# A block of attention, experts and rotation on one core: other loads first, extra products while they run, one add and five columns moved

## The chip, the cores and the metric

The kernel runs on one core of a Trainium2 chip. Five engines of the core work side by side, each with its own instruction stream: TensorE (PE in the profile; PEld is its weight load), VectorE (DVE), ScalarE (ACT), GpSimd (POOL) and SyncE (SP), which here issues transfers. They wait for each other through semaphores. The metric is the device time of one execution in microseconds (us). The time before is 677.72 us, the median of 3 runs (677.05 to 679.04).

## The reference

x has 4 sequences of 512 tokens with 288 channels; cond has one row of 288 for each sequence.

```python
mod = silu(c) @ w_adaln + b_adaln                      # (4, 1728)
sh_msa, sc_msa, g_msa, sh_mlp, sc_mlp, g_mlp = split(mod, 6)
h = ln(x) * (1 + sc_msa) + sh_msa
q, k, v = split(h @ w_qkv + b_qkv)                     # 16 heads of 18
o = softmax(q k^T * 18**-0.5) v @ w_proj + b_proj
x = x + g_msa * o
xn = ln(x) * (1 + sc_mlp) + sh_mlp
cw = softmax over the two largest of xn @ w_gate       # 4 experts
moe = sum_e cw_e * (gelu(xn @ w1_e + b1_e) @ w2_e + b2_e)   # 288 -> 1152 -> 288
x = x + g_mlp * moe
U, _ = qr(P)                                           # P is 288 x 64
R = expm(skew(silu(cond) @ W.T + b))                   # 64 x 64, one per sequence
z = x @ U
out = x + (z @ R - z) @ U.T
```

All of it is computed in float32.

## The kernel before

Everything happens in `fast_path`. The order of the instructions of each engine is the order in which the Python code emits them (a manual schedule), so "behind" on an engine always means later in the code. Each float32 matmul shows as two records (passes) in the profile, each transpose as one.

**Start (L983 to L1100, L2267 to L2285).** SP issues the loads of `cs` (the condition), `wada` (the first 576 columns of w_adaln, 648 KB, one transfer), four tiles of `xs` (the first sequence, 144 KB each), `raw` (part of w_qk, two transfers) and `wadb` (the rest of w_adaln, 1296 KB). ACT's queue issues `badT` (the bias, turned by the host) and the q and k bias. GpSimd fills constants until 6.83 us. `first()` makes the moments of x on DVE (L1180, L1181) and the inverse spread `rs` on GpSimd (L1193, L1194). `shift_scale` makes shift and scale in the layout channel x sequence: for each of the two, 9 products with a 96x96 block of `wada` as weights and 4 columns, into `pm`, and one DVE add into `modT` (L1097); between the two DVE normalizes x (`norm`, L1216). Then ACT compacts two items of w_qk (L1048, L1052); `other_heads` loads the rest of w_qk into the space of `wada`; for each of 3 channel blocks `modulate_T` turns the normalized x with 4 transposes into `pt` (L1229), and ACT applies `modT` into `hT` (L1232); `project` multiplies `hT` by the compacted weights into `pq` (L1787), ACT copies that to `row` (L1829), and SP sends it to `qk`, one transfer for each head (L1834). `values` are the products `pv` (L1750). `qks` are four tiles of 128x2x512, zeroed by DVE, two of them at the very start (L1059).

**Attention (L2428 to L2526).** 32 pairs of steps, 8 for each sequence. A step makes scores `z` (L1865), their exponentials on ACT (L1874) and their products with the values `av` (L1885). A plan hangs other pieces on each pair, in slots `a`, `s` and `b`: the projections of the next sequence, the output projection, the routing, and `column`, the next column of a Householder factorization of P on DVE (`triangular`, L1601 to L1646), 66 pieces in all with the first and the last. Pieces of the matrix exponential (`rotations`, with the squarings L1480, L1530) come one by one beside the pairs. A piece that is a `Split` has a product that `ahead()` can emit before the pair: the first Split of the next pair's `a` and `s` is led so (L2515).

**Experts (L2831 to L2878).** Tokens are sorted by expert into `slots` in two halves; eight expert passes follow, each with `hidden` (L2592, L2605) and `outputs` (L2652), whose rows GpSimd scatters to `chosen` (L2668). At every yield of these, one piece of the list `rest` is emitted: first what is left of the routing, then all columns that are left, then empty steps, then the products that end the factorization (`basis`, L1675 to L1721) with the first half's adds.

**Tail (L2882 to L2892).** Eight pairs of token tiles, four of each half. `Finish.load` reads the two chosen rows of each token (`ycl`, 128x2x2x288 for a pair, 576 KB). `Finish.add` adds them (L2716), multiplies by the gate (L2718) and adds x (L2719), all on DVE; `turn` (L2727), `project_` (L2738) and `store` (L2753, L2761) rotate and write. For pair 4 (`Finish.PAIRS`) loads and adds are cut in two.

Of the kernel before, what the change touches and what calls it, by code (L numbers as in the profile page):

```python
# [10 lines left out]
F32 = mybir.dt.float32  # L11
I32 = mybir.dt.int32
AF = mybir.ActivationFunctionType
ALU = mybir.AluOpType
# [4 lines left out]
P = 128  # L19
# [14 lines left out]
ROOT_SHIFT = float(0x1F3B58D5)  # L34
ROOT_PART = 0.24985


class Split:
    def __init__(self, lead, rest):
        self.lead, self.rest, self.led = lead, rest, None  # L40

    def ahead(self):
# [786 lines left out]
def fast_path(  # L829
# [126 lines left out]
    def bank(shape, name):  # L956

        banks[0] += 1
        if third and banks[0] % 3 == 0:
            return third[0].tile(shape, F32, tag="n", name=name)  # L960
        return ps_m.tile(shape, F32, tag="m", name=name)
# [9 lines left out]
    with ExitStack() as s1:  # L971
# [10 lines left out]
        cs = const.tile([CC, NK, B], F32, name="cs")  # L982
        nc.sync.dma_start(out=cs, in_=cT)  # L983
        wad = w_adaln.rearrange("(k p) f -> p k f", p=CC)
        wada = ada.tile([CC, NK, 2 * C], F32, tag="wa", name="wada")
        nc.sync.dma_start(out=wada, in_=wad[:, :, : 2 * C])
        badT = const.tile([CC, 6, NK], F32, name="badT")
        nc.scalar.dma_start(out=badT, in_=b_adalnT)
        HS = 7
        raw = ada.tile([CC + 1, NK, 2 * HS * HQ], F32, tag="raw", name="raw")  # L990
        braw = raw.rearrange("p k f -> p (k f)")[CC : CC + 1, : 2 * NG * P]
        nc.scalar.dma_start(out=braw, in_=b_qk.rearrange("(o p) t g -> o (p t g)", o=1))
        for t in range(NT):
            nc.sync.dma_start(out=xs[:, t, :], in_=x[0, ts(t, P), :])

# [89 lines left out]
        def shift_scale(between):  # L1085
            pm = bank([P, 2, NK, B], "pm")
            for i in range(2):
                for ch in range(NK):
                    for k in range(NK):
                        nc.tensor.matmul(  # L1090
                            pm[:CC, i, ch, :],
                            wada[:, k, ds(i * C + ch * CC, CC)],
                            sc[:, k, :],
                            start=(k == 0),
                            stop=(k == NK - 1),
                        )
                nc.vector.scalar_tensor_tensor(  # L1097
                    modT[:, i],
                    pm[:CC, i],
                    float(i),  # L1100
                    badT[:, i, :].unsqueeze(2).to_broadcast([CC, NK, B]),
                    ALU.add,
                    ALU.add,
                )
                if i == 0:
                    between()

        VROW = (NH - 1) * (HD + 1) + HQ  # L1110
# [114 lines left out]

        def modulate_T(b, which, xh, k, dst):
            pt = bank([P, N], f"pt{which}{b}{k}")
            for t in range(NT):
                nc.tensor.transpose(  # L1229
                    pt[:CC, ts(t, P)], xh[:, t, ds(k * CC, CC)], ident  # L1230
                )
            nc.scalar.activation(  # L1232
                dst[:CC, k, :],
                pt[:CC, :],
                AF.Identity,
                bias=modT[:, 2 * which, k, b : b + 1],
                scale=modT[:, 2 * which + 1, k, b : b + 1],
            )
# [495 lines left out]
        def begin(b):  # L1734
# [10 lines left out]
            def turn(k):  # L1745
                modulate_T(b, 0, xhs[b], k, hT)

# [15 lines left out]
            def values(pv, t):  # L1763
# [11 lines left out]
                norm,  # L1775
                [lambda k=k: turn(k) for k in range(NK)],
                [Split(lambda t=t: lead(t), lambda pv, t=t: values(pv, t)) for t in range(NT)],
# [491 lines left out]
        first()  # L2269
        shift_scale(norm)  # L2270
        for qk in qks[2:]:
            nc.vector.memset(qk, 0.0)
        compact(0, nc.scalar.copy)
        compact(1, nc.scalar.copy)
        other_heads()
        for piece in turns:
            piece()
        products, sends = project(0, 0, nc.sync)
# [149 lines left out]
        for b in range(B):  # L2428
            at = b * HALF
            last = b == B - 1  # L2430

            for p in {1: (6,), 2: (7,), 3: range(2, 6)}.get(b, range(8)):
                also(at + p, "a", column)
# [37 lines left out]
            also(at + (4 if 0 < b < B - 1 else 6), "a", lambda b=b: residual(b))  # L2471
            for p in {1: (0, 1, 3), 2: (0, 1, 3), 3: (0, 1, 6)}.get(b, ()):
                also(at + p, "b", column)
# [25 lines left out]
        for pair in range(PAIRS):  # L2499
# [15 lines left out]
            if pair + 1 < PAIRS - HALF + 2:  # L2515
                following = plan[pair + 1]["a"] + plan[pair + 1]["s"]
                for piece in [x for x in following if isinstance(x, Split)][:1]:
                    piece.ahead()
# [12 lines left out]
    with ExitStack() as s2:  # L2531
# [148 lines left out]
        class Finish:  # L2680
# [30 lines left out]
            @staticmethod  # L2711
            def add(i):
                yc = Finish.st[i]
                for j, n in ((0, 1), (1, 1)) if i == Finish.PAIRS else ((0, 2),):
                    m, xi = yc[:, ds(j, n), 0, :], xs[:, ds(2 * i + j, n), :]
                    nc.vector.tensor_add(m, m, yc[:, ds(j, n), 1, :])  # L2716
                    g = gates[:, 1, 2 * i // NT, :].unsqueeze(1).to_broadcast([P, n, C])
                    nc.vector.tensor_mul(m, m, g)  # L2718
                    nc.vector.tensor_add(xi, xi, m)  # L2719
# [265 lines left out]
```

## Time and profile before

| what | us |
|---|---|
| median of 3 runs | 677.72 |
| profiled execution | 681.86 |
| its span | 679.9 |
| PE busy | 654.3 |
| PE, first product | 6.84 |
| pq's first pass, pv's first pass | 15.58, 22.09 |
| first scores z | 28.02 |
| last expert product ends, about | 650.2 |
| last PE product starts | 672.45 |

The span runs from the first to the last recorded instruction or transfer of the profiled execution; the time around it is 1.96 us. Busy time counts a pass from its start to its modelled end, so passes overlap. A line of a timeline has start, duration, engine, line of code, operation, output and inputs, and in brackets the idle time before it and what ended it. In a table of windows the columns are the stretch, its length, busy time (with the number of instructions) of PE, PEld, DVE, ACT and POOL, the granted TensorE clock, the busy share of the DMA engines and GB/s.

### The profile page before, as it was taken

How to read it: one execution, taken by the hardware profiler on the slowest of the kernel's cores; microseconds unless marked ns; L12 is line 12 of the kernel's file. 1: busy time of each engine (PE TensorE's matmuls, PEld its weight loads, DVE VectorE, ACT ScalarE, POOL GpSimd, SP SyncE). 2: the span in 40 equal slices, each digit the busy share in tenths (PEclk: the TensorE clock that was granted, in tenths of full speed). 3: DMA queues.
4: the chain of work that ended last, by engine and by line, in shares of the span. 5: the costliest groups of instructions: out<-in, count | busy, mean ns of one | idle time of the engine just before them, and what ended most of it. 6: DMA issues, size and time to landing. Idle time of an engine off the chain costs nothing. (4 is left out here: it accounts for less than half of the span.)

```text
span 679.9 us, 11333 instructions
## 1 busy us (share of the span) xinstructions
PE 654.3 (96%) x3599; PEld 392.0 (58%) x3599; DVE 447.5 (66%) x2000; ACT 293.6 (43%) x469; POOL 245.8 (36%) x388
## 2 busy tenths in 40 slices
PE   5999999999999989999999999999999999999994
PEld 5533344433534334456777757777677676776762
DVE  4443859796699768565978988888888800152135
ACT  4368566765675545733353223232332322312231
POOL 4024688645352485601423653213023031240110
PEclk9999999999999999999999999999999999999999
DMA  9358423233312234461535423644063143550044
GB/s 215 84 164 216 130 86 71 76 106 78 96 56 59 67 112 121 120 164 64 148 70 166 140 96 114 164 136 118 10 183 79 65 132 70 172 158 21 18 150 147
DMA packets 71392, 75.47 MB, mean 111 GB/s; under 512 B 34316, under 2 KB 58610, under 8 KB 71322
## 3 DMA queue, kind: packets, MB, share of 16 engines
q1 hardware_dynamic: 59910, 47.76, 25.3%
q0 software_dynamic: 10912, 26.47, 13.3%
q8 instruction: 30, 0.49, 0.3%
q10 hardware_dynamic: 500, 0.42, 0.3%
q14 instruction: 40, 0.33, 0.2%
HBM read 52.13 MB, written 18.23 MB: 103 GB/s over the span
## 5 line engine op out<-in xcount | busy, mean ns | idle before, releaser
L2652 PE MATMUL pe<-w2s,hm 128*128 128x288 f32 (+1 forms) x648 | 163.8, 408 | 0.0
L1874 ACT ACTIVATE es<-z 128x1024 f32<-128x1024 f32 x128 | 126.0, 1023 | 72.9 <-PE z L1865 66.4
L2592 PE MATMUL ph<-xgT,w1s 128*128 128x288 f32 (+2 forms) x576 | 152.0, 413 | 1.6 <-ACT hm L2614 1.2
L2652 PEld LDWEIGHTS pe<-w2s,hm 128*128 128x128 f32 (+1 forms) x648 | 118.6, 187 | 32.0 <-issue 2.8
L2592 PEld LDWEIGHTS ph<-xgT,w1s 128*128 128x128 f32 x576 | 105.8, 190 | 41.7 <-issue 11.5
L2614 ACT ACTIVATE hm<-ph,b1r 128x576 f32<-128x576 f32 (+2 forms) x72 | 49.9, 737 | 133.6 <-PE ph L2605 121.0
L1865 PE MATMUL z<-qk 32*128 32x512 f32 x512 | 81.0, 647 | 0.6 <-DMA qk<-row 0.6
L2667 POOL TENSOR_TENSOR y<-y,gb 128x288 f32<-128x288 f32 x32 | 28.4, 886 | 140.9 <-ACT y L2666 140.9
L1885 PE MATMUL av<-es,vt 128*32 128x512 f32 x512 | 61.7, 598 | 0.0
L2666 ACT ACTIVATE y<-pe,weight 128x288 f32<-128x288 f32 x32 | 16.0, 500 | 102.7 <-PE pe L2652 99.3
L1787 PE MATMUL pq<-hT,wqk 96*126 96x512 f32 (+4 forms) x156 | 60.2, 519 | 0.0
L2668 POOL DMA_INDIRECT chosen<-y,place x36 | 37.5, 1042 | 52.7 <-DVE y L2664 36.5
L1787 PEld LDWEIGHTS pq<-hT,wqk 97*126 97x126 f32 (+3 forms) x156 | 26.1, 182 | 37.7 <-issue 30.0
L2225 POOL DMA_INDIRECT slots<-xr,where x32 | 32.3, 1009 | 37.7 <-DVE where L2222 24.0
L1610 DVE STREAM_SHUFFLE wj<-pt 32x288 f32<-32x288 f32 (+47 forms) x96 | 42.1, 439 | 0.7
L1865 PEld LDWEIGHTS z<-qk 32*128 32x128 f32 x512 | 24.1, 184 | 28.4 <-ACT es L1874 17.1
L1885 PEld LDWEIGHTS av<-es,vt 128*32 128x32 f32 x512 | 13.5, 109 | 42.8 <-issue 42.8
L1947 PE MATMUL po<-wpg,oraw 128*128 128x288 f32 x128 | 35.8, 420 | 1.8 <-POOL rs L1193 0.9
L1834 POOL DMA_DIRECT2D qk<-row x42 | 21.2, 512 | 36.8 <-ACT row L1829 26.9
L1584 DVE SCALAR_TENSOR_TENSOR pt<-wj,uf,pt 64x288 f32<-64x288 f32 (+62 forms) x63 | 32.7, 519 | 2.2
L1947 PEld LDWEIGHTS po<-wpg,oraw 128*128 128x128 f32 x128 | 23.2, 191 | 18.8 <-issue 9.2
L1599 DVE SCALAR_TENSOR_TENSOR q<-q 64x1 f32<-64x1 f32 (+1 forms) x128 | 29.9, 234 | 4.5
(280 smaller groups left out, 858.2 us busy)
## 6 DMA issues: line engine op xcount, KB each, us to landing
w2s<-in_w_dram SPq DMA_DIRECT2D x8, 1296.0 KB
w1s<-in_w_dram SPq DMA_DIRECT2D x8, 1152.0 KB
slots<-empty POOLq DMA_DIRECT2D x36, 148.0 KB
spread<-rdr SPq DMA_DIRECT2D x64, 64.0 KB
qk<-row POOLq DMA_DIRECT2D x42, 72.0 KB
yc<-chosen SPq DMA_DIRECT2D x4, 576.0 KB
out_dram<-xs SPq DMA_DIRECT2D x8, 288.0 KB
wr<-in_wrT_dram POOLq DMA_DIRECT2D x4, 567.0 KB
```

Source lines behind the costliest of these rows:

```text
L1584: nc.vector.scalar_tensor_tensor(m, w, u[rows, :], m, ALU.mult, ALU.add)
L1610: nc.vector.stream_shuffle(wj[o : o + HQ, j:], pt[o0 : o0 + HQ, j:], [j % HQ] * HQ)
L1787: nc.tensor.matmul(pq[:n, at], wqk[:rows, k, item, :n], hT[:rows, k, at], start=start, stop=(k == NK - 1),)
L1865: nc.tensor.matmul(zs[c // 2][:, c % 2, :], qk[ts(c, HQ), 1, ts(t, P)], qk[ts(c, HQ), 0, :], start=True, stop=True,)
L1874: nc.scalar.activation(e, z, AF.Exp, scale=SCALE)
L1885: nc.tensor.matmul(avs[n][ts(c, HQ), :], vts[b % 2][:, t, ds((4 * g + c) * (HD + 1), HQ)], es[c // 2][:, c % 2, :], start=(t == 0), stop=( ...
L1947: nc.tensor.matmul(po, oTs[NG * b + g][:, ts(t, P)], wpgs[b][:, g, :], start=(g == 0), stop=(g == NG - 1),)
L2225: made = nc.gpsimd.indirect_dma_start(out=slots[h], out_offset=bass.IndirectOffsetOnAxis(ap=where[:, i, t : t + 1], axis=0), in_=xrs[t // ...
L2592: nc.tensor.matmul(ph[:, j, :SB], w1s[:, k, ts(f, P)], xgT[:, k, ts(j, SB)], start=(k == 0), stop=False,)
L2614: nc.scalar.activation(hm[:, f, : CAPS[r]].rearrange("p (j s) -> p j s", j=NB), ph[:, :, :SB], AF.Gelu_apprx_tanh, bias=b1r[:, h, r, f : f ...
L2652: nc.tensor.matmul(po[ts(m, rows), :], slots_[:, f, :], w[:, f, :], start=(f == 0), stop=(f == NF - 1),)
L2668: nc.gpsimd.indirect_dma_start(out=chosen[h], out_offset=bass.IndirectOffsetOnAxis(ap=place[:, t : t + 1], axis=0), in_=y, in_offset=None, ...
```

## The change

Four things change.

1. The four tiles of x are loaded before `wada`; `wada` comes in three transfers, one for each block of 96 input channels; `badT` is replaced by `row01`, a 64x288 tile that DVE zeroes and into which ACT's queue loads the bias of shift (partitions 0 to 3) and scale (32 to 35).
2. `shift_scale` first runs `WARM = 6` products of the identity with a zeroed qk tile, whose results nobody reads; then six products that give shift and scale as rows (32 rows each, sequence x 288 channels); DVE adds the bias row. `turned()` brings the rows into the layout of `modT` with three transposes and one copy. It comes after the first 8 transposes of x. The memsets of the last two qk tiles come behind it. The turns of x become Splits that are not led early in the pairs.
3. Five columns leave the pairs: pair 7 of the third sequence, and pairs 0, 1, 2 and 3 of the fourth. They come in the expert steps behind the other columns.
4. The first add of `Finish.add` runs on GpSimd for pairs 5, 6 and 7.

```diff
+WARM = 6
 class Split:
-    def __init__(self, lead, rest):
+    def __init__(self, lead, rest, early=True):
...
         nc.sync.dma_start(out=cs, in_=cT)
+        for t in range(NT):
+            nc.sync.dma_start(out=xs[:, t, :], in_=x[0, ts(t, P), :])
...
-        nc.sync.dma_start(out=wada, in_=wad[:, :, : 2 * C])
-        badT = const.tile([CC, 6, NK], F32, name="badT")
-        nc.scalar.dma_start(out=badT, in_=b_adalnT)
+        for k in range(NK):
+            nc.sync.dma_start(out=wada[:, k, :], in_=wad[:, k, : 2 * C])
+        row01 = const.tile([2 * HQ, C], F32, name="row01")
+        nc.vector.memset(row01, 0.0)
+        for i in range(2):
+            nc.scalar.dma_start(
+                out=row01[i * HQ : i * HQ + B, :],
+                in_=b_adaln[ds(i * C, C)].partition_broadcast(B),
+            )
...
-        for t in range(NT):
-            nc.sync.dma_start(out=xs[:, t, :], in_=x[0, ts(t, P), :])
...
         def shift_scale(between):
-            pm = bank([P, 2, NK, B], "pm")
-            for i in range(2):
-                for ch in range(NK):
-                    for k in range(NK):
-                        nc.tensor.matmul(
-                            pm[:CC, i, ch, :],
-                            wada[:, k, ds(i * C + ch * CC, CC)],
-                            sc[:, k, :],
-                            start=(k == 0),
-                            stop=(k == NK - 1),
-                        )
-                nc.vector.scalar_tensor_tensor(
-                    modT[:, i],
-                    pm[:CC, i],
-                    float(i),
-                    badT[:, i, :].unsqueeze(2).to_broadcast([CC, NK, B]),
-                    ALU.add,
-                    ALU.add,
-                )
-                if i == 0:
-                    between()
+            one = row01[HQ : 2 * HQ, :]
+            nc.vector.tensor_scalar_add(one, one, 1.0)
+            pm = ps_s.tile([P, 2, N], F32, tag="z", name="pm")
+            for _ in range(WARM):
+                nc.tensor.matmul(
+                    pm[:, 1, :], ident, qks[0][:, 0, :], start=True, stop=True
+                )
+            for k in range(NK):
+                for i in range(2):
+                    nc.tensor.matmul(
+                        pm[ts(i, HQ), 0, :C],
+                        scp[:, k, :],
+                        wada[:, k, ts(i, C)],
+                        start=(k == 0),
+                        stop=(k == NK - 1),
+                    )
+            between()
+            nc.vector.tensor_add(row01, pm[: 2 * HQ, 0, :C], row01)
+
+            def turned():
+                pt = pm[:CC, 1, : NK * 2 * HQ].rearrange("p (k r) -> p k r", k=NK)
+                for k in range(NK):
+                    nc.tensor.transpose(
+                        pt[:, k, :], row01[:, ts(k, CC)], ident[: 2 * HQ, : 2 * HQ]
+                    )
+                nc.vector.tensor_copy(
+                    modT,
+                    pt.rearrange("p k (i r) -> p i k r", i=2)[:, :, :, :B],
+                )
+
+            return turned
...
-        shift_scale(norm)
-        for qk in qks[2:]:
-            nc.vector.memset(qk, 0.0)
+        turned = shift_scale(norm)
         compact(0, nc.scalar.copy)
         compact(1, nc.scalar.copy)
         other_heads()
-        for piece in turns:
-            piece()
+        pts = [turn.lead() for turn in turns[:2]]
+        turned()
+        for qk in qks[2:]:
+            nc.vector.memset(qk, 0.0)
+        for turn, pt_ in zip(turns, pts):
+            turn.rest(pt_)
+        turns[2]()
...
-            for p in {1: (6,), 2: (7,), 3: range(2, 6)}.get(b, range(8)):
+            for p in {1: (6,), 2: (), 3: (4, 5)}.get(b, range(8)):
                 also(at + p, "a", column)
...
-            for p in {1: (0, 1, 3), 2: (0, 1, 3), 3: (0, 1, 6)}.get(b, ()):
+            for p in {1: (0, 1, 3), 2: (0, 1, 3), 3: (6,)}.get(b, ()):
                 also(at + p, "b", column)
...
-                for piece in [x for x in following if isinstance(x, Split)][:1]:
+                for piece in [x for x in following if isinstance(x, Split) and x.early][:1]:
...
-                    nc.vector.tensor_add(m, m, yc[:, ds(j, n), 1, :])
+                    both = nc.gpsimd if i > Finish.PAIRS else nc.vector
+                    both.tensor_tensor(m, m, yc[:, ds(j, n), 1, :], ALU.add)
```

In the built program each wada transfer waits on SP for one earlier transfer to have landed: for `cs`, for the first half of `row01`, and for the first tile of x. The order of the instructions of PE and ACT behind the start is the same as before.

## Prediction

> **What bounds the kernel now.** I read the page's busy times first, then the waits of TensorE, then the start in order of time, then two-microsecond windows around the longest wait in the middle, then the chain that ended last.
>
> ```profile
> PE 654.3 (96%) x3599; PEld 392.0 (58%) x3599; DVE 447.5 (66%) x2000; ACT 293.6 (43%) x469; POOL 245.8 (36%) x388
> ```
>
> TensorE (PE) is busy nearly everywhere: time is won only where it idles or runs slowly. Its three largest waits are the three places that the change touches:
>
> ```profile
> PE pm L1090 <- DMA wada<-in_w_adaln_dram: 6.8, 1, 6.8
> PE pxT L2727 <- DVE xs L2719: 2.8, 3, 1.7
> PE psq L1480 <- DVE XY L1530: 2.3, 1, 2.3
> ```
>
> The start, in order of time (us from the span's start, then the duration):
>
> ```profile
> 11.05 1.45 DVE L1216 TENSOR_SCALAR xh<-xs,mv,rs 128x288 f32<-128x288 f32 x4 [0.99 <-POOL rs L1194]
> ...
> 13.02 2.77 PE L1229 MATMUL pt<-ident,xh 128*96 128x128 f32 x12
> ...
> 15.58 6.67 PE L1787 MATMUL pq<-hT,wqk 97*126 97x512 f32 x12
> ...
> 17.29 0.34 PEld L1787 LDWEIGHTS pq<-hT,wqk 96*126 96x126 f32 x1 [0.52 <-issue]
> 18.14 0.27 PEld L1787 LDWEIGHTS pq<-hT,wqk 96*126 96x126 f32 x1 [0.52 <-issue]
> 18.66 0.19 PEld L1787 LDWEIGHTS pq<-hT,wqk 96*126 96x126 f32 x1 [0.24 <-issue]
> 19.09 0.19 PEld L1787 LDWEIGHTS pq<-hT,wqk 97*126 97x126 f32 x1 [0.24 <-PE pq L1787]
> ```
>
> The reader is to see the spacing of the weight loads: 0.85 us up to 18.14, 0.43 from 18.66. The same 512-column pass runs at half speed until about 18.3. So the 12 passes of pq cost 6.5 us (15.58 to 22.09) instead of 12 x 0.43 = 5.1.
>
> ```profile
> 252.00:254.00 2.00, 0.25 (x6) 0.25 (x8) 1.59 (x7) 0.00 (x0) 1.20 (x3) 0.96 0.20 78
> 254.00:256.00 2.00, 2.00 (x24) 1.16 (x21) 0.00 (x0) 0.00 (x0) 1.67 (x2) 0.50 0.53 163
> 256.00:258.00 2.00, 2.00 (x8) 1.06 (x5) 0.86 (x5) 0.74 (x1) 0.74 (x2) 0.69 0.59 188
> ```
>
> Columns: span, busy PE, PEld, VectorE (DVE), ScalarE (ACT), GpSimd (POOL), granted clock, DMA. PE idles 2.3 us, and the granted clock then falls to 0.50 for 3.4 us (from about 253.85 to 257.25): 1.7 us of work lost on top. What was late is a column of the triangular chain on DVE (from 246.77), with psq's masks behind it:
>
> ```profile
> 246.77 0.45 DVE L1610 STREAM_SHUFFLE wj<-pt 32x271 f32<-32x271 f32 x1
> ...
> 251.25 0.49 DVE L1584 SCALAR_TENSOR_TENSOR pt<-wj,uf,pt 64x271 f32<-64x271 f32 x1
> ...
> 253.21 0.29 DVE L1530 COPY_PREDICATED XY<-need,psq 128x128 f32<-128x128 int32 x1
> ...
> 253.75 1.08 PE L1480 MATMUL psq<-XY 64*64 64x64 f32 x16 [2.29 <-DVE XY L1530]
> ```
>
> The tail is a chain of DVE adds from 661.35, when the first 128x576 load of ycl has landed, to the last turn at 669.67.
>
> **Start.** SP now issues cs, four x tiles, three pieces of wada (one before), then raw. x is issued at 1.28; cs took 1.94 from issue to landing and the x issues are 0.43 to 0.47 apart, so x lands at about 3.8 to 5.5 (up to 6.4 at the pace of wada, 648 KB in 5.4 us). Four pairs of statistics, 0.56 each, end at 6.1 to 7.1. GpSimd's memsets last until 6.83; rs then takes 1.37 (9.64 to 11.01), xh 1.45: ready at about 9.8 instead of 12.5.
>
> PE meanwhile runs six 512-column products, 12 passes. They need the first qk memset, now behind a 64x288 memset (0.3): start 2.5. At half speed a pass costs 0.85, else 0.43; with c us at half speed the twelve last 5.1 + c/2. From pq's start to the rise took 2.7 us; the drop in the middle lasted 3.4, which looks like a fixed window, and a start just after a window's edge would wait for two, 6.8. I take c = 4.5, nearer the middle: end at 9.9 (9.0 to 11.0). Then pm: six 32x288 products, 12 passes, two side by side; the row of the same shape (24 passes, four side by side, 40.1 to 41.3) gives 0.24 a step, 1.45: done 11.35. The last wada piece waits on SP for the first x tile to land, and should land by 8 (bytes ahead of it as before): hidden behind the products. Then eight transposes, 0.14 each as in the tail (0.83 for six): 12.5. DVE's addition of the row (0.45, the row of L1966) lies beside them. Three transposes of the row, a small copy (0.2), modT at 13.1; hT 0.83 (ACT L1232, 2.48 for three); pq from 14.0, at full speed 5.1: ends 19.1 against 22.09. Gain 3.0, of which 1.4 is speed and 1.6 an earlier pq. Bounds: c = 2.7 and ScalarE free at 12.2 after its raw copies, 4.0; c = 6.8 and raw 0.85 late (two more SP issues of 0.42), 0.5. I do not count raw's delay: DMA engines are 0.92 to 1.22 busy from 3 to 19 us, so issue is ahead of transport.
>
> Behind it PE has pv, 5.9 us, and SP seven qk sends that issue 0.78 apart once both rows are copied; both move by 3.0, the fourth send lands about when pv ends, as before. raw2, behind the same bytes, still lands near 19.4; DVE's compaction ends at 22, and its reader pq would start at 26: covered by 4 us.
>
> ACT issues two row01 loads instead of one badT (0.5 more, before the Silu at 2.75, which waits for cs until then): at most 0.3, and PE does not need Silu before 9.9. The 1.0 added to a row, the memsets moved behind modT, and the turns as Split objects that are not led early change no order on PE: nothing.
>
> **Columns.** Five columns of 5.0 us (246.77 to 251.74) leave the stretch from about 212 to 262. The one at 246.77 goes, so XY is ready after den's load, about 250, before PE is free at 251.46: minus 2.3. Without that gap the clock has no reason to drop: minus 1.7 in this profile. Next could be late whatever PE itself feeds; no other PE wait stands there between 241 and 262. They return as 25 us of DVE behind 540, where DVE is busy 4.4 of 20 us and then 0 of 20; if that cover were gone, the R powers from 592 would wait, 5 us at most per column. Bounds: 0 to minus 4.
>
> **Tail.** Three first adds (0.75 on DVE) go to GpSimd. A 128x4 op took 271 ns there and a 128x288 add 790 undisturbed (L2667's shortest), so 128x576 about 1.3. For pair 5 DVE waits for it: plus 0.55. For 6 and 7 it runs beside DVE, and the trace shows what that does:
>
> ```profile
> 597.02 1.44 POOL L2667 TENSOR_TENSOR y<-y,gb 128x288 f32<-128x288 f32 x1 [2.95 <-ACT y L2666]
> ```
>
> Its neighbour on DVE, L2718 at 597.85, took 1.23 instead of 0.76. So a 288-column add costs DVE 0.47, a 576 one twice that, 0.94, unless it falls on an add from PSUM. Queued through: DVE's pair 5 ends 665.2 (663.7 before), pair 6 at 667.85, pair 7 at 670.1 against 669.54: plus 0.5. Without contention: minus 0.75. The Trainium skill, "SBUF — State Buffer", section "SBUF: two separate sides", says more: the port pair is an exclusive lock for the whole instruction, against DVE ops with two SBUF inputs. By it the tail would be plus 1.8 (9.98 us of DVE and GpSimd in a row against 8.19). The trace charges 0.47 of 0.79, so I keep the trace's price.
>
> **Sum.** Profiled execution: 681.86, span 679.9 and 1.96 around it. 681.86 - 3.0 - 2.3 - 1.7 + 0.5 = 675.4. The median of the runs, 677.72, lies 4.1 below the profiled one; the clock's drop may be part of that, so I leave the 1.7 out there: 677.72 - 4.8 = 672.9.
>
> **Rivals.**
> Slower: the products on zeros do not raise the clock. For it: 36 four-column products and nine transposes from 6.84 to 14.9 did not. Then 12 x 0.85 = 10.2 end at 12.7, pm at half speed 15.6, eight transposes of 0.21 17.3, modT 18.4, hT 19.25, pq 6.5: 25.8, plus 3.7. With the rest, 677.72 + 3.7 - 1.8 = 679.6. It turns slower than no change where the start loses over 1.8. Against it: full 512-column passes raised it within 2.7 us.
> The gap in the middle stays, for instance because XY waits for den's load: 675.2.
> The clock falls again before pq, between 11.35 and 14.0, since 2.3 idle us did it at 253.85: pq costs its 1.4 again, 674.3. Against it: the tail keeps 1.0 with 1.3 us idle (662.2 to 663.8). The Trainium skill, "TensorE: Matmul & The Clock Gate", Part 4, says that transposes do not count as busy in the same way, which speaks for the drop; no row isolates them.
> GpSimd blocks DVE for whole adds: 1.3 more than counted, 674.2.
>
> **Chances.** About 0.3% (2 us) is what a measurement can tell from no change. Forecast 0.44, clock falls again 0.12, whole blocking 0.08 and half of the gap that stays (0.12 in all, at the bound of 675.7): faster, 0.70. Its other half 0.06 and other stalls of a start that is moved 0.07: within, 0.13. Zeros that do not warm 0.12 (at the bound of 679.8), other stalls 0.05: slower, 0.17. Range 670.2 (start 4.0, the clock's drop counted) to 678.5; the forecast's own is 671 to 675.
>
> **What would show it.** Right: weight loads of pq 0.43 apart from the first; pq starting near 14 and pv near 19; no wait of psq on XY above 0.5 and no granted 0.50 near 250; GpSimd adds of 1.3 or more in the tail with DVE's L2718 or L2719 over 1.2 beside them. Wrong: the six products lasting 10 us; pm waiting for a wada piece beyond 10; a new PE wait on DVE around 240 to 260, or the R powers starting later against the experts.

## The result, and the profile after

| kernel | median us | lowest to highest | ratio to before (95% interval) |
|---|---|---|---|
| before | 678.93 | 676.61 to 681.50 | |
| changed | 675.13 | 671.27 to 681.27 | 0.9947 (0.9925 to 0.9968) |

The change makes the kernel 0.5% faster: 3.8 us between the medians, 3.6 by the ratio. Forecast were "faster" and a range of 670.2 to 678.5, and both hold. The forecast's own time was 672.9, with 671 to 675 around it; the median lies just above that. The gain was forecast as 4.8 us. The way to the gain was not the forecast's in two of its three parts, and the rest of the document is about those.

The profiled execution of the changed kernel took 675.73, its span 673.7. First its busy line on the page, then its table of TensorE's waits (engine, line, what it waited for, us in all, times, longest).

```profile
PE 654.7 (97%) x3590; PEld 388.0 (58%) x3590; DVE 451.8 (67%) x1999; ACT 294.3 (44%) x469; POOL 250.5 (37%) x391
```

```profile
PE pxT L2754 <- DVE xs L2746: 4.9, 1, 4.9
PE pm L1098 <- DVE qk L1067: 2.4, 1, 2.4
PE ph L1499 <- DVE XY L1537: 1.5, 1, 1.5
```

Of the three waits that the forecast began from, pm's is now 2.4 instead of 6.8, psq's 2.3 is gone, and pxT's, in the tail, has grown from 1.7 to 4.9. A wait of ph, 1.5, which the kernel before had too (1.6), is what remains in the middle.

The start, in order of time (start, duration, engine, line, output and inputs, in brackets the idle time before and what ended it):

```profile
2.45 6.88 PE L1098 MATMUL pm<-qk,ident 128*128 128x512 f32 x12 [2.45 <-DVE qk L1067]
9.26 1.65 PE L1103 MATMUL pm<-wada,scp 96*32 96x288 f32 x12
10.84 1.08 PE L1245 MATMUL pt<-ident,xh 128*96 128x128 f32 x8
11.85 0.37 PE L1116 MATMUL pm<-ident,row 64*96 64x64 f32 x3
...
13.39 5.39 PE L1810 MATMUL pq<-hT,wqk 97*126 97x512 f32 x12 [0.60 <-ACT hT L1251]
19.25 6.07 PE L1773 MATMUL pv<-wv,hT 97*128 97x288 f32 x24 [0.47 <-DMA wv<-in_w_v_dram]
25.25 1.14 PE L1888 MATMUL z<-qk 32*128 32x512 f32 x8
```

It reads as the forecast was written: the twelve passes on zeros end at about 9.3, pq starts at 13.39 (forecast 14.0) and its twelve passes take 5.39 where they took 6.67. The first scores come at 25.25 instead of 28.02.

The middle, in windows of two microseconds around the wait that is left and around the one that went (columns: stretch, length, busy PE, PEld, DVE, ACT, POOL, granted clock, DMA share, GB/s):

```profile
198.00:200.00 2.00, 0.45 (x7) 0.18 (x8) 1.76 (x8) 0.59 (x1) 0.00 (x0) 1.00 0.05 4
200.00:202.00 2.00, 2.00 (x16) 0.70 (x14) 1.93 (x7) 0.00 (x0) 0.00 (x0) 0.50 0.38 111
...
250.00:252.00 2.00, 2.00 (x20) 1.00 (x18) 0.92 (x3) 0.21 (x1) 0.98 (x2) 1.00 0.44 153
252.00:254.00 2.00, 2.00 (x20) 0.41 (x16) 1.98 (x8) 1.53 (x2) 1.70 (x2) 1.00 0.20 76
```

Near 252 TensorE is busy throughout at full clock: gap and fall are gone. (A new wait of 0.35 stands at 247.3, in the middle of a group of scores; the profile names no cause for it.) But the clock fell in this execution at 200, behind ph's 1.5 us wait. In the execution of before the same wait ended at 204.04, and the clock stayed up behind it; its line among the waits and the window behind it are:

```profile
PE ph L1480 <- DVE XY L1518: 1.6, 1, 1.6
204.00:206.00 2.00, 1.96 (x24) 0.84 (x28) 1.93 (x7) 0.32 (x1) 0.00 (x0) 1.00 0.22 76
```

The tail, in order of time, GpSimd, VectorE and TensorE one after the other:

```profile
651.43 4.62 POOL L2743 TENSOR_TENSOR ycl<-ycl 128x576 f32<-128x576 f32 x3 [9.43 <-DMA ycl<-chosen]
...
652.85 1.94 DVE L2745 TENSOR_TENSOR ycl<-ycl,gates 128x576 f32<-128x576 f32 x1 [3.18 <-POOL ycl L2743]
654.82 1.84 DVE L2746 TENSOR_TENSOR xs<-xs,ycl 128x576 f32<-128x576 f32 x1
...
667.10 0.76 DVE L2788 TENSOR_TENSOR xs<-py,xs 128x576 f32<-128x576 f32 x1 [1.22 <-PE py L2780]
...
656.81 1.49 PE L2754 MATMUL pxT<-ident,xs 128*96 128x128 f32 x6 [4.87 <-DVE xs L2746]
658.22 1.33 PE L2780 MATMUL py<-uT,zT 64*128 64x288 f32 x4
659.48 1.50 PE L2765 MATMUL pz<-xT,UR 96*64 96x128 f32 x12
```

The same stretch before, VectorE and TensorE:

```profile
661.35 0.76 DVE L2716 TENSOR_TENSOR ycl<-ycl 128x576 f32<-128x576 f32 x1 [0.94 <-DMA ycl<-chosen]
662.14 0.76 DVE L2718 TENSOR_TENSOR ycl<-ycl,gates 128x576 f32<-128x576 f32 x1
662.93 0.76 DVE L2719 TENSOR_TENSOR xs<-xs,ycl 128x576 f32<-128x576 f32 x1
...
673.26 0.76 DVE L2761 TENSOR_TENSOR xs<-py,xs 128x576 f32<-128x576 f32 x1 [1.26 <-PE py L2753]
...
663.84 0.83 PE L2727 MATMUL pxT<-ident,xs 128*96 128x128 f32 x6 [1.67 <-DVE xs L2719]
```

GpSimd makes its three adds back to back (1.39, 1.39 and 1.76). The two VectorE operations beside them take 1.94 and 1.84, where before each took 0.76. TensorE waits 4.87 for the second, and then works at half clock (a pxT group 1.49 instead of 0.83 to 1.02; the windows from 654 to 660 show 0.50). From the landing of pair 5's load to the last addition the tail took 11.9 us before (661.35 to 673.26) and takes 15.7 here (651.43 to 667.10). The last scatter of the experts was 10.2 us earlier than before (641.01 against 651.26), the end of the span only 6.2.

### The profile page after: what moved, and what is told of

It reads as the page before. It is cut to its first block, busy times and chain, and to the rows that moved or that the text cites. A ratio compares the mean times of both kernels' runs of the same rounds, so it can differ in the third digit from the quotient of the medians.

```text
span 673.7 us, 11329 instructions
## 1 busy us (share of the span) xinstructions
PE 654.7 (97%) x3590; PEld 388.0 (58%) x3590; DVE 451.8 (67%) x1999; ACT 294.3 (44%) x469; POOL 250.5 (37%) x391
## 3 DMA queue, kind: packets, MB, share of 16 engines
q0 software_dynamic: 10912, 26.47, 13.1%
## 4 chain that ended last, share of the span: by engine, by line
PE 87%; DMA 5%; DVE 3%; ACT 1%; SPq 1%; another core or an unknown queue 1%; issue 1%; POOL 0%; DVEq 0%; POOLq 0%; ACTq 0%
PE pe L2678 24%; PE ph L2618 19%; PE z L1888 10%; PE av L1908 8%; PE pq L1810 7%; PE po L1970 5%; PE ph L2631 4%; PE pv L1773 3%; DMA wv<-in_w_v_dram 2%; PE pt L2376 2%; DMA ycl<-chosen 1%; DMA rdr<-den 1%; DMA xs<-in_x_dram 1%; PE psq L1499 1%
## 5 line engine op out<-in xcount | busy, mean ns | idle before, releaser
L2618 PEld LDWEIGHTS ph<-xgT,w1s 128*128 128x128 f32 x576 | 105.8, 190 | 40.8 <-issue 11.4
L1888 PE MATMUL z<-qk 32*128 32x512 f32 x512 | 78.9, 647 | 0.4 <-issue 0.4
L1857 POOL DMA_DIRECT2D qk<-row x42 | 21.3, 514 | 38.3 <-ACT row L1852 28.5
L1600 DVE SCALAR_TENSOR_TENSOR prf<-pt,q,wj 64x288 f32<-64x288 f32 (+62 forms) x63 | 31.2, 495 | 2.2
```

The lines of the kernel that those rows point to most:

```text
L1888: nc.tensor.matmul(zs[c // 2][:, c % 2, :], qk[ts(c, HQ), 1, ts(t, P)], qk[ts(c, HQ), 0, :], start=True, stop=True,)
L2618: nc.tensor.matmul(ph[:, j, :SB], w1s[:, k, ts(f, P)], xgT[:, k, ts(j, SB)], start=(k == 0), stop=False,)
```

## The experiments

They are told in three groups, each measured on one chip against the kernel before on that chip: 679.42 us there for the first four, 677.71 for the second four, 676.59 for the last four. "Landing to end" is from the first 128x576 add, or the first GpSimd add, to the start of the last VectorE addition; "scatter to end" is from the start of the experts' last scatter.

### Each part alone

**The change without GpSimd's adds.**

```diff
-                    both = nc.gpsimd if i > Finish.PAIRS else nc.vector
-                    both.tensor_tensor(m, m, yc[:, ds(j, n), 1, :], ALU.add)
+                    nc.vector.tensor_add(m, m, yc[:, ds(j, n), 1, :])
```

> The changed kernel, but the first add of the tail is on DVE again for pairs 5, 6 and 7. Theory A (the GpSimd adds block DVE for their whole length and cost the tail 3 to 4 us): in the profile the last DVE add starts 12 us after the load of pair 5 has landed, as before (11.9), not 15.7, and the ratio to the kernel before falls from 0.995 to about 0.989 to 0.990. Theory B (the tail lost its time to the phase of the clock alone, not to the adds): the tail stays at 15 us and the ratio near 0.995.

675.99 us (672.27 to 683.94), ratio 0.9945 (0.9922 to 0.9969). In the profile landing to end is 11.9 again, as theory A had it; the ratio of 0.989 to 0.990 that it also had did not come. By the ratios this does not differ from the whole change, which had 0.9947 on another chip: with executions 10 us apart, the tail's price cannot be read from this pair.

The clock fell in this execution too, at 249.6, although psq no longer waits. TensorE, in order of time:

```profile
246.82 1.15 PE L1888 MATMUL z<-qk 32*128 32x512 f32 x4 [0.37 <-issue]
248.27 1.15 PE L1888 MATMUL z<-qk 32*128 32x512 f32 x4 [0.29 <-issue]
249.35 3.90 PE L1970 MATMUL po<-wpg,oraw 128*128 128x288 f32 x8
```

Two waits of 0.37 and 0.29, for which the profile names no cause, stand ahead of it; behind it po takes 3.90 instead of 2.21.

**GpSimd's adds alone**, on the kernel before.

```diff
-                    nc.vector.tensor_add(m, m, yc[:, ds(j, n), 1, :])
+                    both = nc.gpsimd if i > Finish.PAIRS else nc.vector
+                    both.tensor_tensor(m, m, yc[:, ds(j, n), 1, :], ALU.add)
```

> The kernel before with the tail's change alone. Theory A: three GpSimd adds of about 1.5 us, DVE's multiply and add of pair 5 at 1.8 to 2 us instead of 0.76, the wait of PE before turn 5 up from 1.7 to 4 to 5 us, ratio 1.004 to 1.006. The forecast's price of 0.5 us: 1.001. Theory B: 1.000 where the clock does not fall in the tail.

682.22 (681.12 to 685.77), ratio 1.0059 (1.0038 to 1.0080): slower, by 4.0 us after the ratio and 2.8 between the medians. In the profile landing to end is 13.1, 1.2 more than before, and the clock stays up there. TensorE's wait in the tail is 2.6, not the 4 to 5 of theory A. That does not explain 4 us. This execution also has a wait in the middle that the change does not touch, on a transfer that landed late:

```profile
PE po L1947 <- DVE oraw L1926: 3.4, 1, 3.4
PE pxT L2728 <- DVE xs L2720: 2.9, 2, 2.6
```

Before, po's wait was 0.9. So what part of the 0.6% is the tail's stayed open here.

**The columns alone**, on the kernel before.

```diff
-            for p in {1: (6,), 2: (7,), 3: range(2, 6)}.get(b, range(8)):
+            for p in {1: (6,), 2: (), 3: (4, 5)}.get(b, range(8)):
...
-            for p in {1: (0, 1, 3), 2: (0, 1, 3), 3: (0, 1, 6)}.get(b, ()):
+            for p in {1: (0, 1, 3), 2: (0, 1, 3), 3: (6,)}.get(b, ()):
```

> The kernel before with the five columns moved and nothing else. The forecast's theory (a late column starves the squaring): the wait of psq on XY of 2.3 us is gone, and the ratio is 0.994 to 0.997. Rival (the gap was an accident of that run, and the gain in the middle came with the moved start): ratio 0.999 to 1.001.

676.08 (673.39 to 678.04), ratio 0.9939 (0.9917 to 0.9962): 4.1 us by the ratio, 3.3 between the medians. psq no longer waits for XY. Lined up instruction by instruction with the kernel before, TensorE gains 2.4 us at the start of that psq and 1.7 more some ten microseconds ahead of it, where scores had waited for transfers to `qk` (0.57 of it shows as a wait before). In this execution 1.3 us go again inside the same psq, in two waits for which the profile names no cause.

**The start alone**: the change with columns and tail as before.

```diff
-            for p in {1: (6,), 2: (), 3: (4, 5)}.get(b, range(8)):
+            for p in {1: (6,), 2: (7,), 3: range(2, 6)}.get(b, range(8)):
...
-            for p in {1: (0, 1, 3), 2: (0, 1, 3), 3: (6,)}.get(b, ()):
+            for p in {1: (0, 1, 3), 2: (0, 1, 3), 3: (0, 1, 6)}.get(b, ()):
...
-                    both = nc.gpsimd if i > Finish.PAIRS else nc.vector
-                    both.tensor_tensor(m, m, yc[:, ds(j, n), 1, :], ALU.add)
+                    nc.vector.tensor_add(m, m, yc[:, ds(j, n), 1, :])
```

> The kernel before with the change of the start alone (loads, rows, six products on zeros). The forecast's theory: pq starts at 13 to 14 with weight loads 0.43 apart, first scores at 25 instead of 28, ratio 0.9955 to 0.997. Rival (the attention takes the gain back, because loads and columns there do not move along): first scores at 25, but PE waits in the pairs grow and the ratio is 0.999 to 1.001.

678.57 (675.95 to 685.61), ratio 1.0000 (0.9973 to 1.0027). The start itself works: pq ends and z starts 2.2 us earlier than before. At 151 us 0.9 of it is left, at 222 only 0.3. TensorE's waits name where it went:

```profile
PE psq L1499 <- DVE XY L1549: 2.3, 1, 2.3
PE ph L1499 <- DVE XY L1537: 1.3, 1, 1.3
PE po L1970 <- POOL rs L1209: 1.3, 1, 1.3
PE z L1888 <- DMA qk<-row: 1.0, 1, 1.0
```

Before, po's wait on rs was 0.9 and z's on qk 0.6: behind an earlier TensorE the same engines are late by more. In this execution the start's gain becomes waiting time in the attention. (From 397 on the lead is 3.1 again. Of that 1.4 come at 397 itself, where the run of GpSimd's adds alone, whose code there is that of before, gains 0.8 too: the execution of before was late there.) The interval of the ratio still allows a gain or a loss of 1.8 us.

### The zeros and the tail, taken apart

These stand on the change without GpSimd's adds, but for the held clock, which keeps them.

**No products on zeros.**

```diff
-WARM = 6
+WARM = 0
```

> The changed kernel with the tail's adds on VectorE again and without the six products on zeros (WARM = 0). Theory: the products buy the clock alone. Then the shift and scale products, the transposes and the first passes of pq run at half speed, pq starts at 13.4 to 14.5 and its weight loads are 0.85 us apart until the clock has risen, 3 to 4 us later; the first z comes 1.4 to 2.5 us later than with the products (25.25), and the whole is 1.5 to 2.5 us above the same kernel with them. Rival: the earlier x and the rows alone raise the clock in time, because real work is there sooner: z within 0.4 us of 25.25, no difference in the whole.

673.39 (668.5 to 676.75), ratio 0.9938 (0.9904 to 0.9971): no slower. In the profile the row products start at 7.21, as soon as `wada` is there, and the clock rises at 12.9, before pq (13.91); z comes at 25.17. In this execution the theory fell: the zeros bought nothing.

**The clock held in the tail**: the whole change, and five products nobody reads while TensorE waits for pair 5.

```diff
+            if n == PAIRS + 1:
+                held_ = bank_pair("pheld")
+                for _ in range(5):
+                    nc.tensor.matmul(
+                        held_[:, 1, :],
+                        ident,
+                        gates.rearrange("p i b c -> p (i b c)")[:, :N],
+                        start=True,
+                        stop=True,
+                    )
```

> The changed kernel, GpSimd adds and all, with five idle 512-column products put ahead of the turn of pair 5, where TensorE waits for VectorE. From the landing of pair 5's load to the last addition took 11.9 us before and 15.7 us in the changed kernel, of which 654.1 to 660.9 was at half clock. Theory: the wait on VectorE is one part (1.2 us, as with the GpSimd adds alone, 13.1), the clock that the wait lets fall is the other (2.6 us). Then this tail takes 12.8 to 13.6 us with no half clock in it. Rival: the clock is a by-product and VectorE sets the tail by itself: 15 us or more though the clock stays up.

672.21 (670.98 to 673.49), ratio 0.9925 (0.9898 to 0.9953). Landing to end is 13.4 (649.09 to 662.45), with no half clock. GpSimd's two pieces and VectorE's operations beside them:

```profile
649.09 2.76 POOL L2743 TENSOR_TENSOR ycl<-ycl 128x576 f32<-128x576 f32 x2 [9.36 <-DMA ycl<-chosen]
653.29 1.41 POOL L2743 TENSOR_TENSOR ycl<-ycl 128x576 f32<-128x576 f32 x1 [1.44 <-DVE xs L2746]
...
650.52 1.95 DVE L2745 TENSOR_TENSOR ycl<-ycl,gates 128x576 f32<-128x576 f32 x1 [3.07 <-POOL ycl L2743]
653.18 0.75 DVE L2788 TENSOR_TENSOR xs<-py,xs 128x576 f32<-128x576 f32 x1
653.85 1.47 DVE L2745 TENSOR_TENSOR ycl<-ycl,gates 128x576 f32<-128x576 f32 x1
```

Both slow VectorE operations end 0.6 us after GpSimd's (652.47 after 651.85, 655.32 after 654.70), whenever they began: as if they had waited for the whole add and then done their own 0.76. The add from PSUM at 653.18, `xs<-py,xs`, has one input in SBUF and is not slowed. So, by these two executions, of the 3.8 us that the tail lost in the profile of the changed kernel 1.5 are GpSimd's and 2.3 the clock's.

**Contention alone.** VectorE does all the adds; GpSimd does three that nobody waits for.

```diff
+                    if i > Finish.PAIRS:
+                        spare = fin.tile([P, 2, 2, C], F32, tag="yc", name=f"spare{i}", bufs=2)
+                        half = yc[:, :, 1, :]
+                        nc.gpsimd.tensor_tensor(spare[:, :, 0, :], half, half, ALU.add)
```

> VectorE does all the adds of the tail again, and GpSimd does three 128x576 adds from the same loads into a spare tile that nobody reads. No instruction of the chain waits for GpSimd, so what the tail loses is contention alone. Theory (one engine holds the memory port for a whole instruction): VectorE's operations with two inputs in SBUF that meet these adds take 1.8 to 2.0 us instead of 0.76, and the tail, from the landing of pair 5's load to the last addition, takes 13 to 14.5 us against 11.9. The forecast's price (0.47 us for each 288 columns, 0.94 a piece): at most 2.8 us more of VectorE's time, with single operations of 1.2 to 1.7. Rival (the tail lost because VectorE waits for GpSimd's result): VectorE's operations within 0.1 us of 0.76, the tail 11.9.

672.55 (669.58 to 674.37), ratio 0.9918 (0.9891 to 0.9946). Landing to end is 14.0 (650.73 to 664.72):

```profile
650.78 4.95 POOL L2745 TENSOR_TENSOR spare<-ycl 128x576 f32<-128x576 f32 x3 [9.33 <-DMA ycl<-chosen]
...
651.52 1.58 DVE L2748 TENSOR_TENSOR ycl<-ycl,gates 128x576 f32<-128x576 f32 x1
653.14 1.58 DVE L2749 TENSOR_TENSOR xs<-xs,ycl 128x576 f32<-128x576 f32 x1
...
655.31 1.03 DVE L2746 TENSOR_TENSOR ycl<-ycl 128x576 f32<-128x576 f32 x1
```

The rival that VectorE only waits for a result falls: nothing reads these adds, and the tail is 2.1 longer (clock low for 3.4 us of it). The theory's 1.8 to 2.0 for single operations did not come: they took 1.58, 1.58 and 1.03, which the forecast's price would allow too. But each again ended 0.6 us after one of GpSimd's adds (653.10, 654.72 and 656.34 after 652.49, 654.10 and 655.73), which is the theory's waiting and no fixed price. The median is none the less below that of the kernel without these adds (ratio 0.9945, on another chip). Ratios from different chips did not settle a matter of 2 us.

**A sixth column moved** as well, VectorE's adds in the tail.

```diff
-            for p in {1: (0, 1, 3), 2: (0, 1, 3), 3: (6,)}.get(b, ()):
+            for p in {1: (0, 1, 3), 2: (0, 1), 3: (6,)}.get(b, ()):
```

> The changed kernel with the tail's adds on VectorE and a sixth column moved from the attention to the experts, the one that ends at 193 us. Theory: the wait of 1.5 us that TensorE still has at 198 to 200 (ph on XY) goes as the one at 251 went with five, and with it the fall of the clock that follows in some executions: 1.5 us less, 3.2 where the clock fell. Rival: VectorE's queue there is filled by the router's products, not by columns, so the wait stays above 1 us and nothing is won; or a sixth column is too late behind the experts, and the powers of R make TensorE wait up to 5 us near 610.

668.2 (666.42 to 669.11), ratio 0.9864 (0.9836 to 0.9892). ph's wait at 198 is gone, the clock stays up from 7.6 to 663, and between 540 and the tail TensorE waits 0.3 at most, so six columns still have cover there. By ratios from two chips the kernel is 5.5 us faster than the change without GpSimd's adds, more than the 1.5 to 3.2 of the theory. The two profiles lined up give 1.5 at ph, 0.7 more up to 222, and 3.6 between 250 and 262, where the clock had fallen in the other's execution; the theory had no term for the last two. Twelve executions of this kernel and of its repetition below lie between 666.0 and 669.7.

### The parts once more, on the quiet kernel

The kernel with six columns serves as base; each of the others changes one part of it.

**The base, repeated** (no edit).

> The kernel with the earlier start, six columns moved and the tail's adds on VectorE once more, as the base of this row of runs: its executions lay between 666.4 and 669.1 us, a third of the spread of the changed kernel's, since no wait of TensorE over 0.6 us is left between the start and the tail. Theory: that is what makes it tight, and it will be so again, ratio 0.983 to 0.989. Rival: it was the luck of one chip; the executions spread over 10 us as those of the others, and the ratio is nearer to 0.992.

**The base with GpSimd's adds.**

```diff
-                    nc.vector.tensor_add(m, m, yc[:, ds(j, n), 1, :])
+                    both = nc.gpsimd if i > Finish.PAIRS else nc.vector
+                    both.tensor_tensor(m, m, yc[:, ds(j, n), 1, :], ALU.add)
```

> The base with GpSimd doing the tail's three adds, as in the changed kernel: the price of the tail alone where little else varies. Theory: 1.3 us where the clock stays up in the tail (13.1 to 13.4 from landing to the last addition instead of 11.9) and 3.8 where TensorE's longer wait lets it fall (15.7): the median 1.3 to 3.8 us above the base. The forecast: 0.5 us, not to be told from nothing. Rival: in most executions the rounds of the store hide it, a difference below 0.5 us.

**The base without zeros.**

```diff
-WARM = 6
+WARM = 0
```

> The base without the six products on zeros. In the profile of the kernel with five columns the clock rose without them before pq, since the rows' products and the transposes are work enough, and z came at 25.17 instead of 25.25. Theory: the zeros buy nothing, the medians agree within 1 us. Rival (the forecast's step): where the clock's windows fall otherwise, the rise comes only after pq has begun, and the median is 1 to 3 us above the base.

**The kernel before with six columns moved**, which is the base with the start of before.

```diff
-            for p in {1: (6,), 2: (7,), 3: range(2, 6)}.get(b, range(8)):
+            for p in {1: (6,), 2: (), 3: (4, 5)}.get(b, range(8)):
...
-            for p in {1: (0, 1, 3), 2: (0, 1, 3), 3: (0, 1, 6)}.get(b, ()):
+            for p in {1: (0, 1, 3), 2: (0, 1), 3: (6,)}.get(b, ()):
```

> The kernel before with six columns moved and nothing else: the base without its start. Theory: the start's 2.4 to 2.9 us, which the start alone did not show in the time, are kept where no wait on VectorE or ScalarE stands behind them; this kernel lies 2.4 to 3 us above the base, ratio to the kernel before about 0.99. Rival: the attention takes the start's gain back whatever is moved, and this kernel agrees with the base within 1 us.

| kernel | median us | lowest to highest | ratio to before |
|---|---|---|---|
| base again | 666.97 | 666.03 to 669.64 | 0.9848 (0.9806 to 0.9891) |
| with GpSimd's adds | 672.75 | 667.41 to 675.69 | 0.9914 (0.9877 to 0.9952) |
| without zeros | 669.16 | 666.37 to 671.72 | 0.9866 (0.9821 to 0.9911) |
| with the start of before | 669.38 | 668.77 to 670.76 | 0.9879 (0.9837 to 0.9921) |

The base is 1.5% faster than the kernel before, and its executions lie within 3.6 us again.

GpSimd's adds cost 5.8 us between the medians, more than the 3.8 at most that theory gave; by the ratios, whose intervals just overlap, it is 4.5. The profiles agree in kind: scatter to end takes 27.3 us, in the base 21.3. Landing to end is 16.6, 4.7 more than in the base, with the clock at half from 653.5 to 660.3; the other 1.2 are an earlier landing in the base's execution. This is the longest wait it has behind the start (the next is 1.2, po on oraw):

```profile
PE pxT L2754 <- DVE xs L2746: 5.1, 1, 5.1
```

The spread is back too, 8 us.

The start is worth 2.4 us in the medians and 2.1 by the ratios, whose intervals overlap, while the two sets of executions almost do not (666.03 to 669.64, 668.77 to 670.76). The profile with the old start has z at 27.06 and the base's at 25.86; in this one execution of the old start the clock rose two microseconds sooner than in the profile of before (16.4 against 18.3), which pq took as 5.71 instead of 6.67.

The zeros' 2.2 us (1.2 by the ratios) are not told from nothing by these intervals, but the profile without them shows what they can prevent. TensorE, in order of time:

```profile
10.04 1.70 PE L1245 MATMUL pt<-ident,xh 128*96 128x128 f32 x8
...
15.09 8.61 PE L1810 MATMUL pq<-hT,wqk 97*126 97x512 f32 x12 [2.48 <-ACT hT L1251]
```

The clock had risen at 11.4, earlier than in the profile of before. Then `raw` landed late, ScalarE copied it before it could make hT, TensorE waited 2.48, the clock fell at 14.8 for 6.8 us, and pq took 8.61 instead of 5.39. z came at 29.47, later than in the kernel before. With the zeros TensorE comes to that point later. In the profile of the base with GpSimd's adds `raw` was almost as late (ScalarE's second copy of it began at 12.80, here at 13.12), and TensorE waited 0.60; in all eight profiles with the zeros it waited 0.6 to 0.7.

## Why the prediction came out as it did

**Start: right where it stands, but not seen in the time of the changed kernel.** Forecast minus 3.0; the profile of the changed kernel has 2.8 at z. Over all profiles z starts at 25.25 to 25.98 with the products on zeros (eight, 25.60 in the mean) and at 27.06 to 28.02 with the old start (four, 27.63), a gain of 2.0 between the means. In the times, the base lies 2.4 below the same kernel with the old start. The step "I take c = 4.5" measured 3.0 in the changed kernel's execution and 4.5 to 5.9 in the seven others with the products, 4.9 in the mean over all eight: it differs from one execution to the next, within the forecast's bounds of 2.7 to 6.8. The rival that zeros do not raise the clock is out: it rose in all eight while they ran or as they ended. But "1.4 is speed", bought by the zeros, was not shown: without them the row products and transposes raised the clock before pq in both profiles (12.9 and 11.4). What the zeros seem to buy is protection from a second fall, which was the rival "the clock falls again before pq", forecast for the kernel with them and seen in one of two without. What the forecast missed is that the gain need not survive: "other stalls of a start that is moved" had 0.07 (0.12 with the slower ones), and the start alone gained nothing (within 1.8 us).

**Columns: right in place, too small in size.** The forecast left minus 2.3 in the median, and 1.7 more on the profile. The columns alone gave 4.1 by the ratio, 3.3 between the medians. psq's wait went as told: lined up with the profile of before, all eleven profiles with the columns moved gain 2.4 at the start of this psq, and eight of them gain 3.9 from 250 to 262, the forecast's 2.3 and 1.7 together. The other three (the changed kernel, the columns alone, VectorE's adds) lost 1.5 to 3.6 of it again there, in the short waits named above and in the last behind a fall of the clock. The step that was off is "no other PE wait stands there between 241 and 262": the columns leave the stretch from about 212 on, and a wait stood at 240, just ahead of where the forecast looked. All eleven gain 1.7 there; the two others whose columns stand as before do not (minus 0.1 with GpSimd's adds alone, 0.6 with the start alone). Whether the fall of the clock behind the gap was rightly kept out of the median is open. It came in both profiles in which the gap is 2.3 (before, and the start alone, at 253.8 in each); with GpSimd's adds alone the gap was 1.2, and the clock stayed up. So the gap itself differs between executions.

**Tail: wrong.** Forecast plus 0.5; plus 3.8 in the profile of the changed kernel, and on the base plus 5.8 between the medians, 4.5 by the ratios. Two terms failed. First "a 288-column add costs DVE 0.47, a 576 one twice that": the VectorE operations beside a 128x576 add lost between 0.3 and 1.2, by where they had begun. The Trainium skill, "SBUF — State Buffer", section "SBUF: two separate sides", says that the shared ports are locked for a whole instruction when a VectorE operation with two SBUF inputs meets a GpSimd operation that reads SBUF, and that the other fully waits. The runs agree: in five profiles eleven such operations that began during GpSimd's add ended 0.6 us after it, however early they had begun, and an add from PSUM beside it took its usual 0.75. The pair that the forecast read shows the same: its VectorE operation ended at 599.08, 0.6 us after GpSimd's at 598.46. So the 0.47 was where that operation had begun, not the price of an add. The rival of whole blocking had a chance of 0.08 and a tail of plus 1.8 (1.3 more than counted); the lock alone cost 1.2 to 1.5.

Second, and larger: the tail was added up as VectorE's queue, and nothing in the forecast asked what TensorE does meanwhile. With the clock held, VectorE's work for pair 7 ended only 1.0 us later after the landing than before, but the tail's end was 1.5 later: behind pair 5 TensorE works without a wait until its last products, and cannot take up what VectorE wins back. In the changed kernel TensorE's wait grew from 1.7 to 4.9, and the clock fell for 6.8 us behind it; holding the clock gave 2.3 back. (The forecast also read TensorE's idle time in the tail of before as 1.3 us, 662.2 to 663.8; it is 1.67.)

**The sum was right by errors that cancel, which is luck**: 1 to 2 us too little for the columns, 3 to 5 too little for the tail, and a gain of 3.0 for the start that the changed kernel's time does not show. On one chip the start and the columns together (ratio 0.9945) are not faster than the columns alone (0.9939). By their ratios the parts alone make minus 4.1, plus 4.0 and 0.0, in sum nothing (by their medians minus 3.3, plus 2.8 and minus 0.9); together they are minus 3.6. Each ratio is good to 1.4 to 1.8 us, so that the parts do not simply add is likely and not more. Nor do the ratios of the changed kernel, with GpSimd's adds and without (0.9947 and 0.9945, on two chips), show the tail's loss that its profile has.

Where six columns are gone, the start seems to keep its gain. Lined up with the profile of before, the base leads by 2.2 at the end of pq and by 14.3 from 397 on in the experts, the same kernel with the old start by 1.0 and 11.3. That this is because VectorE is no longer behind is argued from the waits of the start's own run, not shown by itself.

The profile of before misled a little: its execution was 4.1 us above the median shown, and other executions of untouched stretches ran faster. With GpSimd's adds alone, which change no code there, TensorE gains 1.05 us on that profile at 111, where po waits for rs, and 0.8 at 397, where ph waits for hm.

## What to carry to other kernels

Work handed to GpSimd is not free for VectorE when both read SBUF: price a meeting by what is left of GpSimd's instruction when VectorE's begins (here 0.3 to 1.2 us lost beside adds of 1.4), and then ask how long TensorE will wait and whether its clock survives. An engine's gain at the start is only as good as the next engine's slack, so clear the waits behind it first; here one more column of VectorE work out of the way was worth as much as the whole change or more, by ratios that compare chips. And compare parts on a version of the kernel whose executions lie close together: those of the base and of the base with the old start lie within 2.0 to 3.6 us of each other, those of the other kernels mostly within 4.6 to 11.7.

## What the runs showed of the hardware

**A wait of 1.55 us can halve TensorE's clock, or not.** The same wait (ph on XY, 1.54 to 1.57) stands in eight profiles; behind it the clock fell for 3.41 us in four (the changed kernel, the columns alone, no zeros, the held tail) and stayed in four (before, VectorE's adds, GpSimd's adds alone, contention alone). Falls and rises within one execution lie whole multiples of 3.413 us apart (in the profile of before 235.52 is 69 of them, 419.84 is 123), and their phase differs from one execution to the next. The Trainium skill, "TensorE: Matmul & The Clock Gate", Part 1, names this free-running window of 3.4 us, and gives idle gaps above 3.4 us as what to avoid; these runs agree on the window, and disagree on the gap, at under half of it. Counting the windows from the clock's rise, the wait lay across two of them in before and with GpSimd's adds alone, where the clock stayed. It lay whole in one in the six others: the clock fell in four and stayed in two (VectorE's adds, contention alone). So what decides is open. It is not the length of one wait alone: with VectorE's adds the clock fell at 249.6 behind waits of 0.37 and 0.29.

**GpSimd and VectorE take turns, and either can wait.** GpSimd's 128x576 add takes 1.39 to 1.41 us with nothing beside it, and the same where a VectorE operation with two inputs in SBUF begins after it and waits. It takes 1.65 to 1.86 where such an operation had begun before it (six adds in four profiles). In these tails, the one that began first kept its time. (At 597 in the profile of before the two began within 0.06 us, and there GpSimd's 128x288 add, the earlier by its record, took 1.44 while VectorE's took 0.74.)

**Products on zeros count as work**: twelve passes on a zeroed tile raised the granted clock 3.0 to 5.9 us after the first, in eight profiles and before any other product.
